# Written slots for the experts' steps of a fused graph-attention and expert layer, and an earlier read of the edge records

## The chip, the core and the metric

The kernel runs on one core of a Trainium2 chip. A core has five engines with an instruction queue each: TensorE (PE, matrix products; its weight loads are counted apart as PEld), VectorE (DVE), ScalarE (ACT), GpSimd (POOL) and SyncE (SP), which here issues most DMAs. Each engine works through its queue in order and waits on semaphores for the others. The metric is the time of one execution on the device, in microseconds; the median of three runs before the change is 6651.61 us (6647.99 to 6666.63).

## The reference

There are N = 30,000 nodes with 256 features and E = 510,000 edges, sorted by destination, each with a type out of 8. One layer is computed:

```
xn   = layernorm(x)
feat = einsum('ni,rhid->rnhd', xn, conv_weights)          # 8 types, 4 heads of 64
e    = leaky_relu(sum(feat[type, src] * attn_l[type]) + sum(feat[type, dst] * attn_r[type]))
h    = segment_softmax(e by dst)-weighted segment_sum of feat[type, src], + h_bias
x    = x + h
y    = layernorm(x)
x    = x + shared(y) + experts(y)
```

`shared` is a network of three layers (256, 128, 256 wide, relu between). `experts` are four networks of three layers (128, 64, 256 wide); a gate picks two of the four for each node by softmax, and their outputs are added with the softmax of the two gate values as weights.

## The kernel before

**The head.** It goes over the nodes in tiles of 128. For each tile VectorE and ScalarE normalise it, TensorE transposes it (`turn`, L292) and multiplies it by all 2048 columns of the weights, plus 64 columns for the attention terms, in pieces of 448 columns (`group`, L305). ScalarE and VectorE copy the pieces out of PSUM (L307), and SP stores a row of 32 x 65 values for each node in `feat` (L319). VectorE's copy of the transposed tile (L294) is what TensorE needs for the tile after the next few pieces.

Between two pieces, twice a tile, `aside()` runs one step of a list of generators: `edge_records` packs source, destination and type of all edges into `rec`; `places` reads these records back, in 21 batches of 12 blocks (`fetch`, L511), sorts out for each partition of a block a first edge, prepares flags and gather indices, and stores them; `expert_weights` loads the experts' weights. A generator gives its turn back at each `yield`. In `places` the first batch is fetched (L522), there is one `yield`, and then the loop fetches batch k + 1 and works on batch k, beginning with VectorE's `key` (L534). A fetch is, for each block, a load of its first edge's number into a register of SP and a DMA that uses it. From three quarters of the tiles on, `first_rows` gathers the first edge's row of each partition of all blocks ahead of time.

**The gather stage.** Edges are cut into 252 blocks of at most 2048 (16 for each of 128 partitions) and a last one of 18 x 128, each of which covers at most 128 destination nodes. For a block GpSimd gathers the edges' rows of `feat`, one indirect DMA for each of 15 places (18 in the last block) and all 128 partitions (L933), into a ring of four blocks in SBUF. There are 3798 such gathers. A gather into a place of the ring waits until TensorE's sums of the block that was there four blocks before are done.

The loop (L1124 to L1169) goes over steps t; a step is cut into NCH = 6 chunks c. In a step the work of several blocks is interleaved: `load` for block t + 2 and `gather` for t + 1 are issued at c = 0; `dest_expand` (TensorE, L987) and `dest_pick` (VectorE, L998 and L1000) bring the destinations' attention terms to block t + 1's edges; `scores` (c = 1), `turn_ends`, `across`, `turn_back` (c = 2, 3, 4), `softmax` and `exps` (c = 5) make block t's softmax; `weigh` (VectorE, L1079) multiplies block t - 1's rows by it, a chunk ahead of `sums` (TensorE, L1086), which adds up the rows by destination through one-hot matrices that ScalarE makes (`onehot`, L1010 and L1011); `finish` (L1104) waits for the sums of c = 5 in that same chunk; `residual_sum` of block t - 2 at c = 0 adds x.

**The experts.** Four blocks of results form a group (T = 4). When its fourth is there, the group's list of steps (`Experts.steps`, L713) is appended to the list `todo`, and each chunk of the loop takes one step from its front (L1157). The 22 steps of a full group, in order: `spread` (the root of the variance, ScalarE); two of `scale` (VectorE); two of `turn` (four transposes on TensorE each, L742, and a copy by ScalarE, L744); `shared1(0)`, `gates`, `shared1(1)`; four of `experts1`, of which the first begins with `choose`, some fifteen small VectorE operations that pick the two experts; `shared2`; two of `experts2`; two of `weigh` (transposes on TensorE, a product on VectorE); `turn_gates`; four of `last` (16 matrix products in all, a sum on VectorE and a store by SP for each). A layer is four instructions of 512 columns on TensorE (L798) and a relu on ScalarE (L799). A step may return a piece that is run at the start of the next chunk, through the list `late`. A group lasts 24 chunks, so before the change steps lie in chunks 0 to 21 of it, and 22 and 23 are free.

The order inside each engine's queue is the order in which this Python code calls the instructions (`manual_schedule`); no scheduler moves them.

Of the kernel before, what the change touches and what calls it, by code (L numbers as in the profile page):

```python
# [40 lines left out]
T = 4  # L41
# [12 lines left out]
def kernel(  # L54
# [121 lines left out]
    for i in range(NPEN + 1):  # L176
        f = wf.tile([P, H, U if i < NPEN else UL], F32, name=f"penf{i}")
# [44 lines left out]
    with ExitStack() as cx:  # L222
# [268 lines left out]
        def places(cl):  # L491
# [19 lines left out]
            def fetch(k):  # L511
                if k == len(batches):
                    return
                b0, n = batches[k]
                rc = rcs[k] = kp.tile([P, GB, UW, 4], I32, name="rcb")
                for b in range(n):
                    lo = nc.values_load(lo_sb[0:1, b0 + b:b0 + b + 1], engines={SP}, min_val=0, max_val=E)
                    r = rec[ds(lo, CAP), :].rearrange("(p u) f -> p (u f)", u=U)
                    nc.sync.dma_start(rc[:, b].rearrange("p u f -> p (u f)"),
                                      bass.AP(tensor=r.tensor, offset=r.offset, ap=[[4 * U, P], [1, 4 * UW]]))  # L520

            fetch(0)  # L522
            yield
            done = None
            for k, (b0, n) in enumerate(batches):
                fetch(k + 1)
# [99 lines left out]
        with tc.manual_schedule():  # L626
# [27 lines left out]
            while slot < 16:  # L654
                attention(slot, ab)
                slot += 1
            cl.close()
            side = [edge_records(cl), places(cl), expert_weights()]
            ahead = first_rows()

# [41 lines left out]
    class Experts:  # L702
# [8 lines left out]
        def steps(self):  # L711
            return ([self.spread] + [lambda j=j: self.scale(j) for j in (0, 2)]
                    + [lambda k=k: self.turn(k) for k in range(2)]  # L713
                    + [lambda: self.shared1(0), self.gates, lambda: self.shared1(1)]
                    + [lambda e=e: self.experts1(e) for e in range(NE)]
                    + [self.shared2] + [lambda i=i: self.experts2(i) for i in range(2)]
                    + [lambda i=i: self.weigh(i) for i in range(2)]
                    + [self.turn_gates] + [lambda t=t: self.last(t) for t in range(self.n)])

        def stats(self, t):  # L720
            st = self.pool.tile([P, 6], F32, name="c_st")
            nc.vector.bn_stats(st[:M], self.x1[:M, t, :])
            nc.vector.bn_aggr(self.mv[:M, t, :], st[:M])
# [138 lines left out]
    with ExitStack() as cx:  # L862
# [16 lines left out]
        NCH = 6  # L879
# [207 lines left out]
                                 s.ft[:, u].rearrange("p h d -> p (h d)"), start=u == 0, stop=u == s.u - 1)  # L1087

        groups = {}
        todo = []  # L1090
        late = []

        def put(t, rows_t):

            if t < NBLK:
                n0 = nc.values_load(n0_sb[0:1, t:t + 1], engines={SP}, min_val=0, max_val=N - P)
                nc.sync.dma_start(out[ds(n0, P), :], rows_t)
            else:
                nc.sync.dma_start(out[N - P:N, :], rows_t)
# [9 lines left out]
        def residual_sum(t):  # L1109
            s = blk.pop(t)  # L1110
            q, j = divmod(t, T)
            n = min(T, NBLK + 1 - q * T)
            if j == 0:
                x1 = x1p.tile([P, T, D], F32, name="x1")
                groups[q] = Experts(xc, ph_p, pc_p, x1, n, lambda i, r, q=q: put(q * T + i, r))
            x1 = groups[q].x1
            nc.vector.tensor_add(x1[:, j, :], s.ho.rearrange("p h d -> p (h d)"), s.xt)
            groups[q].stats(j)
            if j == n - 1:
                todo.extend(groups.pop(q).steps())  # L1120

        with tc.manual_schedule():  # L1124
            for t in range(-2, NBLK + 12):
                def at(f, b, *a):
                    if 0 <= b <= NBLK:
                        f(b, *a)
                for c in range(NCH):
                    while late:  # L1130
                        late.pop()()
                    if c == 0:
                        at(load, t + 2)
                        at(gather, t + 1)
                        at(flags, t + 1)
                    if c == 1:
                        at(flags_across, t + 1)
                    if c == 2:
                        at(turn_ends, t)
                    if c == 3:  # L1140
                        at(across, t)
                    if c == 4:
                        at(turn_back, t)
                    if c == 5:
                        at(softmax, t)
                        at(exps, t)
                    if c < NCH - 1:
                        at(weigh, t - 1, c + 1)
                    if c < 4:
                        at(dest_pick, t + 1, c)  # L1150
                    if c == 0:
                        at(residual_sum, t - 2)
                    if c == 1:
                        at(scores, t)
                    if c == 4:
                        at(dest_select, t + 2)
                    if todo:  # L1157
                        after = todo.pop(0)()
                        if after:
                            late.append(after)  # L1160
                    if c == 5:
                        at(weigh, t, 0)
                        at(dest_expand, t + 2, 0)
                    if c < 3:
                        at(dest_expand, t + 1, c + 1)
                    at(onehot, t, c)
                    at(sums, t - 1, c)
                    if c == 5:
                        at(finish, t - 1)  # L1169
            assert not todo and not groups and not late  # L1170


    again = nc.values_load(bad[0:1, 0:1], min_val=0, max_val=1)
# [187 lines left out]
    with ExitStack() as cx:  # L1361
# [3 lines left out]
        with tc.For_i(0, again * NQ) as q:  # L1365
# [7 lines left out]
            for step in g.steps():  # L1373
                after = step()
# [30 lines left out]
```

## Time and profile before

| | us |
|---|---|
| timed, median of 3 | 6651.61 |
| profiled execution | 8380.65 |
| its span | 8379.0 |
| last matrix product of the head ends | 1746 |
| first gather of the gather stage starts | 1750.45 |
| last gather starts | 8259.83 |

| engine | busy us in the span | share |
|---|---|---|
| TensorE | 6330.2 | 76% |
| VectorE | 5381.4 | 64% |
| GpSimd | 4073.5 | 49% |
| ScalarE | 3416.7 | 41% |

The profile is of one execution, and this one took 1729 us longer than the timed median. Its mean granted TensorE clock is 0.877. Busy time is the time in which an engine had an instruction running; the ends of matrix products are modelled. In lines of instructions in order of time the columns are start, duration (both us), engine, source line, operation, output and inputs, count, and in brackets the idle time before it with what ended it; "issue" stands for a wait that the profile doesn't explain, "remote" for one whose signal isn't matched to an instruction. In a row of a group, what stands behind the bar is busy time, mean ns of one instruction, idle time of the engine just before them, and what ended most of it. In the table of waits the columns are the total in us, how often, and the longest.

### The profile page before, as it was taken

What the parts mean: (1) busy time and instruction counts of PE and PEld (TensorE: products, weight loads), DVE (VectorE), ACT (ScalarE), POOL (GpSimd) and SP (SyncE); (2) the same over time, 40 slices, a digit from 0 to 9 for tenths busy, and PEclk for the clock granted to TensorE, in tenths of its full rate; (3) what the DMA queues carried; (4) which work ended last, traced back from release to release, by engine and by line L of the source; (5) the groups of instructions that cost most, each with busy time, mean ns of one, the idle gap of its engine ahead of it and who ended that gap; (6) DMA issues with size and microseconds to landing.
All of it is one profiled execution on the core that took longest, in us unless ns stands there. A gap on an engine that the chain in (4) does not pass through costs nothing. (4 is left out here: it accounts for less than half of the span.)

```text
span 8379.0 us, 96556 instructions
## 1 busy us (share of the span) xinstructions
PE 6330.2 (76%) x25254; PEld 3986.0 (48%) x25255; DVE 5381.4 (64%) x13882; ACT 3416.7 (41%) x9511; POOL 4073.5 (49%) x4327
## 2 busy tenths in 40 slices
PE   9999999956666767777666667777666777777667
PEld 5555555534444444444444444444444444444444
DVE  5557774447666666666666666666666666666665
ACT  2222222224444444444444444444444444444444
POOL 1101114665555555555555555555555555555552
PEclk9999999978888888888888888888888888888888
DMA  6657778964444444444444444444444444444441
GB/s 226 229 177 238 224 243 303 341 197 123 116 117 117 118 116 119 119 121 119 117 120 117 119 116 118 118 123 118 118 116 117 118 119 118 116 119 117 115 118 55
DMA packets 761457, 1209.52 MB, mean 144 GB/s; under 512 B 241638, under 2 KB 599789, under 8 KB 730685
## 3 DMA queue, kind: packets, MB, share of 16 engines
q1 hardware_dynamic: 565453, 663.56, 24.8%
q0 software_dynamic: 194400, 539.40, 23.3%
q8 instruction: 206, 3.38, 0.2%
q14 instruction: 358, 2.93, 0.1%
q10 hardware_dynamic: 1040, 0.26, 0.0%
HBM read 818.57 MB, written 384.23 MB: 144 GB/s over the span
## 5 line engine op out<-in xcount | busy, mean ns | idle before, releaser
L933 POOL DMA_INDIRECT ft<-feat,rk x3798 | 3608.6, 950 | 2919.9 <-PE po L1086 956.0
L1086 PE MATMUL po<-ft,oh 128*128 128x260 f32 x8100 | 2305.4, 421 | 286.3 <-DVE ho L1107 149.5
L1086 PEld LDWEIGHTS po<-ft,oh 128*128 128x128 f32 x8100 | 1565.4, 208 | 569.7 <-issue 292.4
L305 PE MATMUL ps<-w,xT 128*128 128x448 f32 (+1 forms) x4700 | 1712.6, 519 | 14.3 <-DVE xT L294 8.6
L1079 DVE TENSOR_TENSOR ft<-ft,p 128x768 f32<-128x768 f32 x1518 | 1289.9, 850 | 394.8 <-issue 184.1
L1010 ACT ACTIVATE oh<-icol,rk 128x128 f32<-128x128 f32 x4032 | 1329.1, 389 | 66.4 <-remote 45.5
L305 PEld LDWEIGHTS ps<-w,xT 128*128 128x128 f32 x4700 | 877.3, 191 | 704.9 <-issue 613.5
L798 PE MATMUL ph<-xT,w 128*128 128x512 f32 (+1 forms) x512 | 372.1, 859 | 961.8 <-issue 888.7
L307 ACT COPY fo<-ps 128x448 f32<-128x448 f32 (+1 forms) x711 | 377.3, 533 | 1087.4 <-PE ps L305 912.4
L998 DVE TENSOR_TENSOR ere<-pe,rk 128x384 f32<-128x384 f32 x1008 | 553.3, 549 | 373.4 <-remote 247.9
L1011 ACT ACTIVATE oh<-oh 128x384 f32<-128x384 f32 x1518 | 740.2, 488 | 49.4
L987 PEld LDWEIGHTS <-ohT 128*128 128x128 bf16 x4050 | 393.9, 158 | 548.8 <-issue 438.1
L798 PEld LDWEIGHTS ph<-xT,w 128*128 128x128 f32 x512 | 112.3, 260 | 1112.1 <-issue 952.5
L744 ACT COPY xT<-ph 128x512 f32<-128x512 f32 (+1 forms) x128 | 73.1, 572 | 1325.3 <-remote 1299.9
L1000 DVE TENSOR_REDUCE e<-ere 128x16 f32<-128x384 f32 (+1 forms) x1012 | 561.5, 555 | 34.8
L987 PE MATMUL pe<-erp,ohT 128*128 128x96 bf16 x4050 | 442.3, 236 | 113.3 <-DVE ohT L970 73.5
L798 PE MATMUL ph<-xT,v 128*128 128x512 f32 (+1 forms) x1024 | 500.2, 613 | 2.3 <-ACT h L799 1.5
L1062 DVE TENSOR_TENSOR c<-t,rk 128x128 f32<-128x128 f32 x252 | 71.8, 285 | 618.9 <-remote 582.0
L1071 ACT ACTIVATE p<-e 128x64 f32<-128x64 f32 (+1 forms) x253 | 70.4, 278 | 844.9 <-DVE e L1022 741.8
L307 DVE COPY fo<-ps 128x448 f32<-128x448 f32 (+1 forms) x464 | 242.3, 528 | 221.9 <-PE ps L305 194.2
L1040 PE MATMUL t<-ident,fb 128*4 128x128 f32 x253 | 70.8, 280 | 383.6 <-DVE fb L1033 196.7
L851 PE MATMUL pf<-w,h 128*128 128x256 f32 x506 | 203.2, 491 | 189.1 <-ACT wT L844 85.1
(206 smaller groups left out, 7422.2 us busy)
## 6 DMA issues: line engine op xcount, KB each, us to landing
feat<-fo SPq DMA_DIRECT2D x234, 1040.0 KB
dr<-dk_d SPq DMA_DIRECT2D x252, 516.0 KB
ft<-feat,rk POOLq DMA_INDIRECT x3798
stage<-fr SPq DMA_DIRECT2D x63, 520.0 KB
ft<-stage SPq DMA_DIRECT2D x252, 130.0 KB
xt<-xb_d SPq DMA_DIRECT2D x253, 128.0 KB
out_dram<-og SPq DMA_DIRECT2D x253, 128.0 KB
xb_d<-xb SPq DMA_DIRECT2D x58, 512.0 KB
```

The costliest lines, as they stand in the source:

```text
L305: nc.tensor.matmul(ps, t["xT"][:, k, :], w[:, k, c0:c1], start=k == 0, stop=k == 1)
L307: eng(t["fo"][:, h0:h1, :HD], ps[:, :n].rearrange("p (a d) -> p a d", d=HD))
L798: nc.tensor.matmul(ps[:, :self.w], lhs, rhs, start=i == 0, stop=i == len(pairs) - 1)
L851: nc.tensor.matmul(pf[:M], self.h2[:, tok], w3, start=True, stop=False)
L933: nc.gpsimd.indirect_dma_start(out=s.ft[:, u].rearrange("p h d -> p (h d)"), out_offset=None, in_=feat[:, :], in_offset=bass.IndirectOffse ...
L987: nc.tensor.matmul(pe[:, u - u0].rearrange("p f r -> p (f r)"), s.ov[:, u, :], s.erp.rearrange("n h k r -> n (h k r)"), start=True, stop=True)
L998: nc.vector.tensor_mul(ere, s.pe[:, :u1 - u0], s.th[:, u0:u1, None, :].to_broadcast([P, u1 - u0, H * 3, R]))
L1000: nc.vector.tensor_reduce(s.e[:, :, u0:u1].rearrange("p h u -> p u h"), ere.rearrange("p u (h k) r -> p u h (k r)", h=H), AX.X, ALU.add)
L1010: nc.scalar.activation(s.oh[:, u, :], icol, AF.Abs, bias=s.nd[:, u:u + 1])
L1011: nc.scalar.activation(s.oh[:, u0:u1], s.oh[:, u0:u1], AF.Relu, bias=1.0, scale=-1.0)
L1079: nc.vector.tensor_mul(fc, fc, pc[:, :, None].to_broadcast([P, (u1 - u0) * H, HD]))
L1086: nc.tensor.matmul(s.po.rearrange("n h d -> n (h d)"), s.oh[:, u, :], s.ft[:, u].rearrange("p h d -> p (h d)"), start=u == 0, stop=u == s. ...
```

## The change

Three edits:

- `places` gives its turn back six times instead of once between the fetch of the first batch and the first use of its records.
- A group's steps are no longer taken from a list one by one. `Experts.SLOTS` names a chunk for each of the 22 steps, counted from the chunk in which the group is complete. The chunks 3, 6, 17, 20, 22 and 23 have no step of this group. The four steps of the last layer are in chunks 24 to 27, which are chunks 0 to 3 of the next group: in 0, 1 and 2 they share the chunk with that group's `spread` and two `scale`, behind these. `plan` holds for each chunk of the loop the steps that are due; `free` keeps a later group (the last one, of a single block) from starting before 24 chunks have passed since the one before it.
- The pieces in `late` are run first in, first out instead of last in, first out.

```diff
@@ places
             fetch(0)
-            yield
+            for _ in range(6):
+                yield
             done = None
@@ class Experts
+        SLOTS = (0, 1, 2, 4, 5, 7, 8, 9, 10, 11, 12, 13, 14, 15, 16, 18, 19, 21, 24, 25, 26, 27)
+
@@
         groups = {}
-        todo = []
+        plan = {}
         late = []
+        free = [0]
@@ residual_sum
             if j == n - 1:
-                todo.extend(groups.pop(q).steps())
+                first = free[0] = max((t + 2) * NCH, free[0])
+                free[0] += T * NCH
+                for i, f in zip(Experts.SLOTS, groups.pop(q).steps()):
+                    plan.setdefault(first + i, []).insert(0, f)
@@ the loop
                     while late:
-                        late.pop()()
+                        late.pop(0)()
@@
-                    if todo:
-                        after = todo.pop(0)()
+                    for f in plan.pop(t * NCH + c, ()):
+                        after = f()
                         if after:
                             late.append(after)
@@
-            assert not todo and not groups and not late
+            assert not plan and not groups and not late
```

## The prediction

> **What bounds the kernel now.** I read the page first, then the stages, then GpSimd's instructions in order of time, then who waited for whom.
>
> The page: span, engines, and the costliest group.
>
> ```profile
> span 8379.0 us, 96556 instructions
> PE 6330.2 (76%) x25254; PEld 3986.0 (48%) x25255; DVE 5381.4 (64%) x13882; ACT 3416.7 (41%) x9511; POOL 4073.5 (49%) x4327
> L933 POOL DMA_INDIRECT ft<-feat,rk x3798 | 3608.6, 950 | 2919.9 <-PE po L1086 956.0
> ```
>
> No engine is full over the whole span, and the profiled execution (8380.65 us) is 1729 us longer than the timed median (6651.61). So before anything is costed, I must know where those 1729 us are. The row of L933 tells: 3798 gathers, each 0.95 us busy, and 2919.9 us of idle time in front of them. GpSimd's own instructions in order of time show how much of that idle time belongs to the gather itself:
>
> ```profile
> 1750.45 0.95 POOL L933 DMA_INDIRECT ft<-feat,rk  x1 [18.19 <-DMA stage<-fr]
> 1751.70 0.95 POOL L933 DMA_INDIRECT ft<-feat,rk  x1 [0.30 <-issue]
> 1752.96 0.95 POOL L933 DMA_INDIRECT ft<-feat,rk  x1 [0.30 <-issue]
> ...
> 8258.58 0.95 POOL L933 DMA_INDIRECT ft<-feat,rk  x1 [2.06 <-PE po L1086]
> 8259.83 0.94 POOL L933 DMA_INDIRECT ft<-feat,rk  x1 [0.30 <-issue]
> ```
>
> Nothing delays the second and third, and they start 1.25 us after the one before: 0.95 us and 0.30 us of issue. First to last gather is 8259.83 - 1750.45 = 6509 us; 3797 x 1.2525 = 4756 us of it is gathers without a wait, 1754 us is waiting. That is the missing 1729 us, within 25. So the timed execution has next to none of these waits: gather stage = 4756 us of GpSimd issue + about 25 us. With the head (1750 us) and the tail (8379 - 8260 = 119 us) as profiled, 1750 + 4756 + 119 + 2 around the span = 6627; the rest to 6651.6 is those 25 us. If the tail is shorter when timed (it holds some of the stalls below; 80 us would be my estimate), the waits left are up to 64 us.
>
> The waits that inflate the profile sit behind the experts' transposes. The table of waits:
>
> ```profile
> ACT xT L744 <- remote: 1299.9, 63, 22.3
> PE ph L798 <- issue: 889.1, 60, 16.7
> DVE c L1062 <- remote: 582.0, 61, 20.3
> ```
>
> 63 is the number of groups of four blocks: once a group ScalarE waits about 20 us for a transpose whose record ended long before. If that were in timed runs too, a group would take what it takes in the profile (6509 / 252 x 4 = 103.3 us); timed it is (6651.6 - 2 - 1750 - 119) / 252 x 4 = 75.9 us. VectorE alone is busy 4209.33 us of the 6300 between 1900 and 8200, or 69.0 us a group; with two waits of some 10 us in front of it (582 / 61, and those on PSUM at L998) it would be at 83. So these stalls belong to the profiled execution.
>
> The head is another regime. The busy time by stages (columns: stretch, its length, busy us and instructions of TensorE, its weight loads, VectorE, ScalarE, GpSimd; then granted clock, DMA share, GB/s):
>
> ```profile
> 570.00:580.00 10.00, 3.93 (x12) 1.90 (x10) 0.38 (x1) 0.19 (x1) 0.00 (x0) 0.94 0.17 31
> 580.00:590.00 10.00, 7.48 (x17) 3.77 (x18) 9.13 (x24) 1.94 (x5) 0.00 (x0) 0.72 0.16 30
> 590.00:600.00 10.00, 10.00 (x32) 5.58 (x31) 6.68 (x20) 2.44 (x6) 4.33 (x8) 1.00 0.82 313
> ```
>
> TensorE, then VectorE, in order of time at this gap:
>
> ```profile
> 569.68 4.25 PE L305 MATMUL ps<-w,xT 128*128 128x448 f32 x12
> 582.52 4.81 PE L305 MATMUL ps<-w,xT 128*128 128x448 f32 x8 [8.60 <-DVE xT L294]
> ...
> 579.62 0.50 DVE L534 SCALAR_TENSOR_TENSOR key<-rcb,iu 128x192 f32<-128x192 int32 x1 [12.35 <-DMA rcb<-rec]
> ```
>
> Else TensorE is busy 10.00 of 10 us at clock 1.00: it sets the head. Here VectorE stands 12.35 us at the first use of the records that `fetch(0)` reads, the copy of xT (L294) is queued behind, and TensorE runs dry for 8.60 us and comes back at a clock of 0.72.
>
> **What the Trainium skill says.** "DMA: Bandwidth & Descriptors", SWDGE vs HWDGE vs iDMA: descriptors of DMAs issued from GpSimd are computed by its own cores in software. The trace agrees: 0.95 us of GpSimd for each gather, whatever else runs. "Perfetto Trace Analysis", Tensor Engine Instruction: the end of a matmul's record is an estimate, not an observation; that fits ScalarE's wait of 20 us after a transpose that looks finished. "TensorE: Matmul & The Clock Gate", Part 1: TensorE's clock falls to half after an idle window of some 3.4 us; the stage above shows 0.72 after the gap of 8.60 us.
>
> **The change part by part.**
>
> Records six steps ahead. Nothing is added to any queue; the first batch's VectorE work comes five steps later than before, so the fetches of batch 1 on SP do too. Steps come twice a tile and a tile of the head takes 7.31 us (transposes at 547.53, 554.84, 562.15), so the first batch reaches VectorE 2.5 x 7.31 = 18 us later, from about 571 to 589. Its records are there at 579.6: cover of 9 us. Gain: 8.60 us of idle, and the slow restart (8 records in 4.81 us where 20 take 7.26, so 4.81 - 2.90 = 1.91). Together 10.5 us, and all of it reaches the end, since TensorE is full to its last matmul (1746) and the first gather starts at 1750.45, behind the last store. Bounds: 10.5 gained, or 0 if the wait only goes to another DMA. Everything after shifts by 18 us: the batches end near 1280 instead of 1262, the expert weights' loads near 1330, and TensorE is still busy with the head until 1746, so the cost is nothing; if that cover were gone it would be those 18 us.
>
> The experts' slots. 22 steps a group before and after, with the same instructions: spread, scales at slots 0, 1, 2 as before; the transposes go from 3, 4 to 4, 5; the first layer from 5 to 7; the last layer's four steps from 18 to 21 to 24 to 27, which are slots 0 to 3 of the next group. No gather moves, and nothing is put in GpSimd's queue. SP's stores of the output move with the last layer by six slots, so they stay at the same four places inside a step, behind the loads for the block two ahead that are issued at its start; a store that waits on VectorE there can hold up only the next step's loads, which have a whole step of 18.8 us in hand. So the path (60 gathers x 1.2525 = 75.2 us a group) loses and gains nothing directly. What it can lose is only waits: a gather waits until the sums of the block four before are done (ring of four blocks). Those are the 25 us (at most 64) of the timed run. What the slots do to the engines behind: the last layer (TensorE 1.7 us a step by its 8 records of some 0.22 us) now lies beside the scales (VectorE 0.41 x 4 = 1.65 us), slots heavy on one engine beside slots heavy on the other; and slot 5, where `finish` waits on VectorE for the sums of the same slot, has a transpose (0.44 us at that pace) in place of a 512 wide layer (1.9 us). I estimate 1 to 2 us a group less waiting on VectorE, in work that mostly follows GpSimd. I take 40% of the 25 us: 10 us gained. Bounds: 64 gained (every wait goes), and a loss as under the rivals.
>
> The order in which late pieces are run (first in, first out) changes nothing while one waits at a time, as here. The tail: the last groups run 36 steps after the blocks' work instead of 35, but four pairs of them overlap: 0, within 3 us.
>
> Sum: 6651.6 - 10.5 - 10 = 6631 us.
>
> **Rivals.**
>
> Compute and not GpSimd sets the timed pace. For it: VectorE's 69.0 us a group plus four waits for the exponentials (the timeline shows 1.7 us in front of the first weighting) come to 75.8, as near to the measured 75.9 as GpSimd's 75.2. Against it: the waits of the profile account for the whole difference only if they are nearly absent when timed. Then the slots' 1 to 2 us a group count up to GpSimd's limit, 0.7 us a group or 45 us, at most 64: 6651.6 - 10.5 - 45 = 6596.
>
> Slower: the doubled slots. In slot 1 VectorE now has the late sum of the last layer (0.42), weighting (0.68), pick (1.10), scores (1.75) and scale (0.83), and TensorE's next last layer waits for that late sum, since its PSUM tile has one buffer. If this delays transposes of scores, then `across`, softmax, the exponentials and the sums that free the ring, the group grows. GpSimd hides it until the group passes 75.2 us, from 72.6 (69.0 and 3.6 of small gaps, my estimate); beyond 2.6 us every us costs 63. At 3.4 us: +50, less 10.5: 6691.
>
> No difference: the wait on the first records turns into one on the next batch, and the ring hides the slots: 6651.
>
> **How the numbers follow.** GpSimd's pace with the head's gap gone: 0.45, 6615 to 6645 with 6631 in it. Compute's pace: 0.20, 6580 to 6615. Slower: 0.20, 6660 to 6710. No difference: 0.15, 6645 to 6658. About 0.3% (20 us) is what a measurement of this kernel can tell from no change; the three runs before lie within 18.7 us. Faster by more than that is below 6631.7: half of the first case and the second, 0.43. Slower is above 6671.6: most of the third, 0.18. Between: 0.39. The range of 8 in 10, 6590 to 6690, leaves out the ends of the second and third case.
>
> **What would show it.** In the profile after: TensorE has no gap between 560 and 600 us; the first gather starts near 1740; gathers without a wait still start 1.25 us apart; the time from the last gather to the end stays within 10 us of 119. The waits behind transposes can shrink or move by hundreds of us in the profiled execution; by my reading the timed median doesn't follow. If it follows, or falls under 6580, GpSimd is not what paces the timed run and the step on the 1729 us is wrong. If the median is over 6670, the doubled slots have passed the ring's cover.

## The result and the profile after

| | us |
|---|---|
| timed after, median of 4 (6773.13 to 6776.68) | 6774.7 |
| timed before, median of 4 (6647.99 to 6666.63) | 6652.67 |
| ratio | 1.018, interval 1.0162 to 1.0198 |
| profiled execution after | 6775.31 |
| its span | 6773.6 |

The change makes the kernel 1.8% slower; 6631 was predicted, with a range from 6590 to 6690. The profile of before that stands further up is of an execution that took 8380.65 us, so what is compared here is a second profile of the same kernel (the first experiment below), with a span of 6669.8 us, which is called undisturbed.

From the page of after: the span, the engines, and the costliest group (busy us and mean ns; then idle time in front of it).

```profile
span 6773.6 us, 96498 instructions
PE 5995.3 (89%) x25254; PEld 3855.3 (57%) x25255; DVE 5344.5 (79%) x13882; ACT 3435.3 (51%) x9511; POOL 4068.8 (60%) x4327
L938 POOL DMA_INDIRECT ft<-feat,rk x3798 | 3605.6, 949 | 1349.2 <-issue 448.8
```

The same three lines of the kernel before, undisturbed:

```profile
span 6669.8 us, 96556 instructions
PE 6002.1 (90%) x25254; PEld 3849.3 (58%) x25255; DVE 5352.6 (80%) x13882; ACT 3425.9 (51%) x9511; POOL 4069.6 (61%) x4327
L933 POOL DMA_INDIRECT ft<-feat,rk x3798 | 3606.7, 950 | 1236.2 <-issue 446.6
```

No engine's busy time differs by more than 10 us, and TensorE's mean granted clock is 0.963 in both. What has grown is the idle time in front of the gathers: 113 us more (1349.2 against 1236.2). The first gather starts 12 us earlier, and from the last gather to the end it takes 3 us longer, which makes the 104 us between the two spans. The gathers are where the loss shows; the runs below tell that it doesn't come from them. The table of waits (total us, times, longest us), first of after, then of the kernel before:

```profile
ACT xT L749 <- PE ph L747: 446.4, 65, 11.2
DVE ft L1084 <- ACT ft L1077: 370.7, 253, 2.2
POOL ft L938 <- PE po L1091: 320.0, 866, 4.1
```

```profile
POOL ft L933 <- PE po L1086: 305.6, 1003, 0.3
ACT xT L744 <- PE ph L742: 192.6, 65, 10.2
DVE ft L1079 <- ACT ft L1072: 181.3, 253, 1.0
```

VectorE waits for the exponentials once a block in both (253 blocks), but 370.7 us in all instead of 181.3. That is 189 us more, on the engine with the most work after TensorE. ScalarE also waits longer for the transposes (446.4 against 192.6), and one of these longer waits stands in front of an exponential, as the next lines show.

The gap of the head is gone. The busy time by stages (columns as in the prediction), after:

```profile
570.00:580.00 10.00, 10.00 (x31) 5.36 (x30) 5.36 (x17) 3.02 (x7) 0.47 (x1) 1.00 0.26 70
580.00:590.00 10.00, 10.00 (x31) 5.52 (x31) 5.39 (x17) 1.90 (x4) 0.00 (x0) 1.00 0.81 304
```

TensorE is busy 10.00 of 10 us at clock 1.00 where it had 4.57 and 6.80 us in the undisturbed kernel before. The first gather starts at 1733.3 us instead of 1745.4 ("near 1740" was reckoned from the 1750.45 of the first profile).

**Where VectorE's wait grows.** In every fourth block (the one whose chunk 4 is slot 4 of the group), instructions in order of time of after: TensorE, then VectorE, then ScalarE.

```profile
3422.54 0.69 PE L859 MATMUL pf<-b,wT 17*128 17x256 f32 x2
3424.68 0.22 PE L1060 MATMUL t<-ident,carf 4*128 4x4 f32 x1
3424.89 0.66 PE L747 MATMUL ph<-ident,c_xn 128*128 128x128 f32 x4
...
3420.88 0.38 DVE L1053 TENSOR_TENSOR_SCAN carb<-through,t 4x128 f32<-4x128 f32 x1
3424.20 1.28 DVE L975 TENSOR_SCALAR ohT<-dr,rowid 128x2064 bf16<-128x2064 int16 x1
3427.09 0.22 DVE L1027 TENSOR_REDUCE e<-m 128x4 f32<-128x64 f32 x1
3429.54 0.95 DVE L1084 TENSOR_TENSOR ft<-ft,p 128x768 f32<-128x768 f32 x1 [2.22 <-ACT ft L1077]
...
3425.58 0.59 ACT L749 COPY xT<-ph 128x512 f32<-128x512 f32 x1 [6.79 <-PE ph L747]
3426.07 0.98 ACT L1015 ACTIVATE oh<-icol,rk 128x128 f32<-128x128 f32 x3
3427.08 0.53 ACT L1016 ACTIVATE oh<-oh 128x384 f32<-128x384 f32 x1
3427.63 1.28 ACT L1076 ACT_TABLE_LOAD   x1
3428.92 0.28 ACT L1076 ACTIVATE p<-e 128x64 f32<-128x64 f32 x1
```

VectorE has the scores less their maximum (L1027) at 3427.31, the end of that line. ScalarE is not ready for them: it has waited 6.79 us for the transposes, then copies them, makes one-hot matrices and loads the table of the exponential, in the order of its queue, and starts the exponential at 3428.92. VectorE stands 2.22 us. The same place in the kernel before:

```profile
3403.73 0.22 PE L1055 MATMUL t<-ident,carf 4*128 4x4 f32 x1
3403.94 0.66 PE L742 MATMUL ph<-ident,c_xn 128*128 128x128 f32 x4
...
3402.34 0.38 DVE L1048 TENSOR_TENSOR_SCAN carb<-through,t 4x128 f32<-4x128 f32 x1
3405.13 1.28 DVE L970 TENSOR_SCALAR ohT<-dr,rowid 128x2064 bf16<-128x2064 int16 x1
3408.02 0.22 DVE L1022 TENSOR_REDUCE e<-m 128x4 f32<-128x64 f32 x1
3408.95 0.95 DVE L1079 TENSOR_TENSOR ft<-ft,p 128x768 f32<-128x768 f32 x1 [0.71 <-ACT ft L1072]
...
3404.63 0.58 ACT L744 COPY xT<-ph 128x512 f32<-128x512 f32 x1
3406.67 1.28 ACT L1071 ACT_TABLE_LOAD   x1
3408.27 0.28 ACT L1071 ACTIVATE p<-e 128x64 f32<-128x64 f32 x1 [0.32 <-DVE e L1022]
```

The same chain on ScalarE is there, and as long: from the transposes at 3403.94 to the exponential at 3408.27 it takes 4.3 us, against 4.0 after. But here VectorE comes to its part later still, and ScalarE waits for it (0.32). What has moved is TensorE: it begins `turn_back` (L1060) 3.4 us after VectorE finished `across` (L1053; median over the groups), where it was 1.0 us before, since the last layer (L859) of the previous group now lies in the chunks just ahead. In that time VectorE gets ahead: its `dest_select` (L975) begins 0.48 us before `turn_back`, where it began 1.40 us behind it before. So from the start of `turn_back` VectorE needs only 2.6 us to the end of L1027, while the chain on ScalarE, which stands behind the same late `turn_back`, needs 4.2 us to reach the exponential.

The second place is the block whose chunk 4 is slot 16, where the change puts the second `experts2` (before: slot 14). ScalarE, then VectorE, after:

```profile
3466.03 0.69 ACT L830 ACTIVATE a<-ph,c 128x512 f32<-128x512 f32 x1
3466.61 0.61 ACT L834 COPY wide<-wt 128x512 f32<-128x512 f32 x1
3467.12 0.99 ACT L1015 ACTIVATE oh<-icol,rk 128x128 f32<-128x128 f32 x3
3468.14 0.52 ACT L1016 ACTIVATE oh<-oh 128x384 f32<-128x384 f32 x1
3468.57 0.27 ACT L1076 ACTIVATE p<-e 128x64 f32<-128x64 f32 x1
...
3466.82 0.22 DVE L1027 TENSOR_REDUCE e<-m 128x4 f32<-128x64 f32 x1
3469.18 0.95 DVE L1084 TENSOR_TENSOR ft<-ft,p 128x768 f32<-128x768 f32 x1 [2.14 <-ACT ft L1077]
```

The scores are there at 3467.04 (the end of L1027); a relu and a copy of 512 columns (0.69 and 0.61 us) have come into the queue in front of the one-hots and the exponential, which starts 1.53 us late.

Over all groups VectorE's wait for the exponentials, by the block's number modulo 4, is 0.72, 0.72, 0.71, 0.72 us in the kernel before and 0.72, 2.22, 0.87, 2.13 after: 3.07 us more a group. VectorE's time of a group, put together from its instructions, gaps under 0.3 us, and waits:

| kernel | busy | small gaps | waits | group |
|---|---|---|---|---|
| before, undisturbed | 68.60 | 3.41 | 4.61 | 76.6 |
| six yields, old list | 68.52 | 3.41 | 4.32 | 76.3 |
| after | 68.44 | 3.36 | 6.69 | 78.5 |

78.5 - 76.3 = 2.2 us a group (3.07 for the exponentials and 0.5 for the gates' product more, 1.2 for the last layer less, and 0.1 less of busy time and gaps). 63 x 2.2 = 140 us; measured between those two spans: 6773.6 - 6636.6 = 137 (6636.6 is the span of the run with six yields, below).

TensorE is nearly as busy as VectorE in this stage: between 1900 and 6300 us of the undisturbed kernel before, 87.8% against 89.5%. But VectorE waits for TensorE's products only 1.7 us of the 76.6 of a group, while TensorE stands idle 7.4 us for VectorE and 1.9 for ScalarE. No run takes work from either of the two. That VectorE and not TensorE sets the pace rests on these waits, and on the last two runs, in which VectorE is held up or not while TensorE's work stays the same.

### The profile page after: what moved, and what is told of

Read it like the earlier page. It is cut to its first block, busy times and chain, and to the rows that moved or that the text cites. A ratio compares the mean times of both kernels' runs of the same rounds, so it can differ in the third digit from the quotient of the medians.

```text
span 6773.6 us, 96498 instructions
## 1 busy us (share of the span) xinstructions
PE 5995.3 (89%) x25254; PEld 3855.3 (57%) x25255; DVE 5344.5 (79%) x13882; ACT 3435.3 (51%) x9511; POOL 4068.8 (60%) x4327
## 5 line engine op out<-in xcount | busy, mean ns | idle before, releaser
L938 POOL DMA_INDIRECT ft<-feat,rk x3798 | 3605.6, 949 | 1349.2 <-issue 448.8
L1091 PE MATMUL po<-ft,oh 128*128 128x260 f32 x8100 | 2236.4, 411 | 343.0 <-ACT ends L960 169.6
L1091 PEld LDWEIGHTS po<-ft,oh 128*128 128x128 f32 x8100 | 1513.7, 201 | 728.8 <-ACT ends L960 351.9
L1084 DVE TENSOR_TENSOR ft<-ft,p 128x768 f32<-128x768 f32 x1518 | 1288.7, 849 | 370.7 <-ACT ft L1077 370.7
L1016 ACT ACTIVATE oh<-oh 128x384 f32<-128x384 f32 x1518 | 740.4, 488 | 48.1
L803 PE MATMUL ph<-xT,v 128*128 128x512 f32 (+1 forms) x1024 | 482.2, 594 | 1.9 <-ACT h L804 1.5
L992 PE MATMUL pe<-erp,ohT 128*128 128x96 bf16 x4050 | 426.2, 230 | 53.9 <-DVE ohT L975 48.1
L294 DVE COPY xT<-ptr 128x256 f32<-128x256 f32 x229 | 97.0, 424 | 370.6 <-PE ptr L292 368.7
L804 ACT ACTIVATE h<-ph,b 128x512 f32<-128x512 f32 x192 | 131.0, 682 | 433.2 <-PE ph L803 430.4
L616 POOL DMA_INDIRECT fr<-feat,lowc x252 | 239.2, 949 | 171.2 <-issue 68.9
L975 DVE TENSOR_SCALAR ohT<-dr,rowid 128x2064 bf16<-128x2064 int16 (+1 forms) x253 | 324.1, 1281 | 3.4 <-DMA feat<-fo 2.9
L803 PE MATMUL ph<-xT,w 128*128 128x512 f32 (+1 forms) x512 | 311.7, 743 | 0.2 <-ACT xT L749 0.2
L274 POOL TENSOR_TENSOR xb<-xg,hb 128x1024 f32<-128x1024 f32 (+1 forms) x59 | 141.8, 2403 | 276.6 <-DMA xg<-in_x_dram 162.0
L749 ACT COPY xT<-ph 128x512 f32<-128x512 f32 (+1 forms) x128 | 74.6, 584 | 446.4 <-PE ph L747 446.4
```

The costliest lines, as they stand in the source:

```text
L803: nc.tensor.matmul(ps[:, :self.w], lhs, rhs, start=i == 0, stop=i == len(pairs) - 1)
L938: nc.gpsimd.indirect_dma_start(out=s.ft[:, u].rearrange("p h d -> p (h d)"), out_offset=None, in_=feat[:, :], in_offset=bass.IndirectOffse ...
L975: nc.vector.tensor_scalar(ohT[:, :3 * s.dw].rearrange("n (i e) -> n i e", i=3), s.dr[:, :, :s.dw], rowid[:, t:t + 1], None, op0=ALU.is_equal)
L992: nc.tensor.matmul(pe[:, u - u0].rearrange("p f r -> p (f r)"), s.ov[:, u, :], s.erp.rearrange("n h k r -> n (h k r)"), start=True, stop=True)
L1016: nc.scalar.activation(s.oh[:, u0:u1], s.oh[:, u0:u1], AF.Relu, bias=1.0, scale=-1.0)
L1084: nc.vector.tensor_mul(fc, fc, pc[:, :, None].to_broadcast([P, (u1 - u0) * H, HD]))
```

## The experiments

Theory A, formed on these traces: VectorE's queue paces the gather stage, and GpSimd's 75.2 us a group lie just below it. What ScalarE or TensorE have in chunk 4 ahead of the exponentials lengthens it. Theory B is that of the prediction: GpSimd paces, with room for VectorE, or (its slower rival) the doubled slots, those with steps of two groups, cost as such.

### The kernel before, and the head alone

First, before without any edit. 

> The kernel before, unchanged, for a second profiled execution. Theory A (the 20 us behind the transposes belonged to that one execution, and in the timed runs VectorE and GpSimd are close to each other): the span falls to about 6650 us, once a group no wait of 20 us is left, and VectorE is busy or in front of the weighting of the exponentials nearly all the time, in 75.6 us a group. Rival B (the long waits belong to the kernel under the profiler): the span is again near 8380 us.

Measured 6671.49 us, with the profile shown above. Its gathers take 4823.3 us from the first to the last, 67.6 more than 3797 x 1.2525. The 1754 us of waits that the prediction read from its profile are not in an undisturbed execution.

```diff
@@ before, places
-            yield
+            for _ in range(6):
+                yield
```

> The kernel before with the records read six steps ahead alone. The first gather of the changed kernel starts at 1733 us and not 1750, so if the head is independent of the experts' slots: 6653 - 17 = 6636 us. If the head's gap was part of the disturbed execution only: 6653 us.

Measured 6649.68 against 6660.79, ratio 0.9985 (0.9979 to 0.9992): 11 us gained. The head's part of the prediction (10.5) holds; the 17 us of the expectation were reckoned from the first gather of the first profile.

```diff
@@ after, places
-            for _ in range(6):
-                yield
+            yield
```

> The changed kernel with a single step between the first fetch and its use, so the slots alone. If the two parts add up, and the slots cost all of the loss: 6775 + 10 to 17 = 6785 to 6792 us. If the earlier read costs something in the gather stage, less than 6775 us.

Measured 6785.25, ratio 1.0187 (1.017 to 1.0204). The slots alone cost 124 us; less the 11 us of the head that is 113, and the change, against the same 6660.79, costs 114. The two parts add up.

### Which slots

```diff
@@ after
-        SLOTS = (0, 1, 2, 4, 5, 7, 8, 9, 10, 11, 12, 13, 14, 15, 16, 18, 19, 21, 24, 25, 26, 27)
+        SLOTS = (0, 1, 2, 4, 5, 7, 8, 9, 10, 11, 12, 13, 14, 15, 16, 17, 18, 19, 20, 21, 22, 23)
```

> The changed kernel with slots 0, 1, 2, 4, 5 and then 7 to 23 without a hole: free slots behind the scales and the transposes, the last layer in 20 to 23, nothing beside the next group's first steps. Theory A (ScalarE late for the exponentials: the second experts2 stands at chunk 4, with a relu and a copy in front of the exponentials, and VectorE waits there 2.13 us where 0.72 is the least, in one block of four, some 90 us in all): slow as the changed kernel, 6720 to 6775 us. Theory B (the doubled slots 0 to 3 cost): fast, 6630 to 6660 us.

Measured 7119.71, ratio 1.0687 (1.0669 to 1.0705), which neither theory had expected. The table of waits of this kernel names a new one, VectorE's sum waiting for the last layer's product:

```profile
DVE og L862 <- PE pf L859: 362.6, 191, 9.2
DVE ft L1084 <- ACT ft L1077: 269.2, 253, 2.2
```

The wait for the exponentials at slot 4 is down to 0.72 us although the transposes are in slots 4 and 5 as in the change; only the one at slot 16 stays (2.12). TensorE begins `turn_back` there 0.4 us after `across`. So the wait at slot 4 needs both, transposes there and the last layer ahead of them. But the last layer in chunks 2 to 5 of the fourth block costs much more (a group of 84.1 us, 5.5 of it in the wait of the first line). Why TensorE is so late with it was not tried further and stays open.

```diff
@@ after: the second experts2 out of chunk 4
-        SLOTS = (0, 1, 2, 4, 5, 7, 8, 9, 10, 11, 12, 13, 14, 15, 16, 18, 19, 21, 24, 25, 26, 27)
+        SLOTS = (0, 1, 2, 4, 5, 7, 8, 9, 10, 11, 12, 13, 14, 15, 17, 18, 19, 21, 24, 25, 26, 27)
```

> The changed kernel with its second experts2 in slot 17 in place of 16, so behind the exponentials of chunk 5 on ScalarE and not before them. Theory A (ScalarE is late for the exponentials in two of four blocks, and VectorE, which has no slack, pays): the wait in front of the first weighting of that block falls from 2.13 to 0.72 us, 1.41 us x 63 groups = 89 us: 6775 - 89 = 6686 us, the other late block stays at 2.22. Rival (the doubled slots set the loss, or GpSimd does): 6755 to 6795 us.

Measured 6723.73, ratio 1.0095 (1.0076 to 1.0114), 51 us less than after where A had 89. The wait at slot 16 fell from 2.13 to 0.83, nearly as expected, but `gates` waits for its product 0.6 us a group longer (1.10 against 0.53), and the group is 77.6 us; 0.6 x 63 = 38 us is what is missing from the 89. Why that wait grew is not shown.

```diff
@@ after: the transposes back to 3 and 4
-        SLOTS = (0, 1, 2, 4, 5, 7, 8, 9, 10, 11, 12, 13, 14, 15, 16, 18, 19, 21, 24, 25, 26, 27)
+        SLOTS = (0, 1, 2, 3, 4, 7, 8, 9, 10, 11, 12, 13, 14, 15, 16, 18, 19, 21, 24, 25, 26, 27)
```

> The changed kernel with the two transposes in slots 3 and 4 as in the kernel before. Theory A1 (the slot number of the transposes makes ScalarE late): the wait of 2.22 us falls to 0.72, 1.5 x 63 = 95 us: 6680 us. Theory A2 (TensorE is late in slot 4 because the last layer now stands in slots 0 to 3, so the second transposes' copy still stands late in front of the exponentials): the wait stays near 2.2 us, and the time at 6760 to 6790 us.

Measured 6785.47, ratio 1.019 (1.0171 to 1.0209), 11 us more than the change. One of the two transposes is still in chunk 4, and the waits are 2.22 and 2.12 as in the change.

```diff
@@ after: transposes at 3 and 5, the second experts2 at 17
-        SLOTS = (0, 1, 2, 4, 5, 7, 8, 9, 10, 11, 12, 13, 14, 15, 16, 18, 19, 21, 24, 25, 26, 27)
+        SLOTS = (0, 1, 2, 3, 5, 7, 8, 9, 10, 11, 12, 13, 14, 15, 17, 18, 19, 21, 24, 25, 26, 27)
```

> The changed kernel with the transposes in slots 3 and 5 and the second experts2 in 17, so that no step of slots 4 and 16 has work on ScalarE in front of the exponentials; the last layer stays beside the next group's first steps. Theory A: both waits fall to 0.72 us, 2.9 us a group: 78.5 - 2.9 = 75.6 us a group, 6775 - 183 = 6592 us, under the kernel with six yields alone (6650). If the doubled slots cost by themselves: 6650 to 6700 us.

Measured 6621.34, ratio 0.9938 (0.9919 to 0.9958). With chunk 4 clear in both blocks the waits are 0.72, 0.73, 0.90 and 0.83 us and the loss becomes a gain, though 29 us short of what was expected: a group takes 76.1 us and not 75.6, and 0.55 us of it is VectorE waiting for the last layer's product, which the change didn't have.

```diff
@@ after: the old list of steps, only the last layer moved
-        SLOTS = (0, 1, 2, 4, 5, 7, 8, 9, 10, 11, 12, 13, 14, 15, 16, 18, 19, 21, 24, 25, 26, 27)
+        SLOTS = (0, 1, 2, 3, 4, 5, 6, 7, 8, 9, 10, 11, 12, 13, 14, 15, 16, 17, 24, 25, 26, 27)
```

> The changed kernel with slots 0 to 17 without holes, as before the change, and only the last layer moved to 24 to 27. Theory A2: the second transposes in slot 4 come late behind the last layer of slots 0 to 3, VectorE waits some 1.5 us longer for the exponentials there, and saves the 1.2 us a group that it waits for the last layer before: +0.3 us a group, 6650 + 20 = 6670 us. If moving the last layer is free of cost: 6650 - 77 = 6573 to 6595 us. If the doubled slots cost all of the loss: 6775 us.

Measured 6669.65, ratio 1.0019 (1.0012 to 1.0025). Against the six yields alone, the overlap with a transpose left in slot 4 costs 20 us: the wait there is 2.22 again, the others 0.72. TensorE begins `turn_back` 3.85 us after `across`, with nothing but the last layer moved.

### Is it GpSimd, and is it the place in ScalarE's queue?

```diff
@@ six yields, old list: one gather a block left out, from the fifth block on
-            for u in range(1 if s.own else 0, s.u):
+            for u in range(1 if s.own else 0, s.u - (s.own and t >= RING)):
```

> The kernel with six yields (old list of steps), in which each block from the fifth on leaves out the gather of its last place; that place keeps what an earlier block left in the ring, so the sums are those of wrong rows, while every other instruction stays. 248 gathers less, 248 x 1.2525 = 311 us of GpSimd's issue, and 3.75 us less in front of each block. If GpSimd's gathers pace the timed stage (the prediction's step on the 1729 us): 6650 - 311, about 6340 us, or down to where VectorE's 68.5 + 3.4 us a group come next. If VectorE's queue with its waits for the exponentials paces it (theory A): the time stays, 6635 to 6655 us, with GpSimd idle near 26 us a group in place of 21.

```diff
@@ the last layer over (as above): the second transposes and all between one chunk later
-        SLOTS = (0, 1, 2, 3, 4, 5, 6, 7, 8, 9, 10, 11, 12, 13, 14, 15, 16, 17, 24, 25, 26, 27)
+        SLOTS = (0, 1, 2, 3, 5, 6, 7, 8, 9, 10, 11, 12, 13, 14, 15, 16, 17, 18, 24, 25, 26, 27)
```

> The changed kernel with the slots 0, 1, 2, 3, 5, 6 ... 18, 24, 25, 26, 27: the last layer overlaps as in the change, the second transposes leave slot 4 (free), the second experts2 is at 15, not in the fifth chunk of a block. Theory A (VectorE's queue, lengthened when ScalarE's or TensorE's work of chunk 4 stands in front of the exponentials): all four waits for the exponentials fall to 0.72 us, the late sums of the last layer wait less, a group takes 75.3 to 76.0 us against 76.6 of before, so 6585 to 6625 us. Doubled slots as such are the cost (the prediction's rival): no better than the change, 6740 us or more. If GpSimd's 75.2 us a group is the floor it can't go under 6585 us.

Beside these two the kernel before took 8441.34 us in seven timed runs (8428.21 to 8442.98), about as long as the execution that the prediction read; the two kernels took 8339.04 (0.9858, 0.9817 to 0.99) and 8340.2 (0.9878, 0.9859 to 0.9898). The expectations were for 6660 us of before, so neither can be judged by these times. Both kernels were run again, on another chip.

> The same kernel as in the run on which the kernel before took 8441 us: six yields, old list of steps, the gather of the last place left out from the fifth block on (the sums there are those of wrong rows). Where the kernel before takes some 6660 us: if GpSimd's gathers pace the stage, 6650 - 311 = 6340 us or down to VectorE's need; if VectorE's queue with its waits for the exponentials paces it, the time stays at 6635 to 6655 us.

Measured 6654.21 against 6660.88, ratio 0.999 (0.9981 to 1.0); with six yields and all gathers it is 6649.68. 311 us of GpSimd's work are gone and the time stays. The page's row of the gathers, and their wait in the table of waits:

```profile
L934 POOL DMA_INDIRECT ft<-feat,rk x3550 | 3371.9, 950 | 1457.8 <-issue 407.6
```

```profile
POOL ft L934 <- PE po L1087: 397.0, 912, 8.3
```

From the first gather to the last it takes 4809.7 us, with all gathers 4804.0. In excess of 1.2525 us a gather that is 364.6 us instead of 48.3: GpSimd now waits for about as long as it no longer works, up to 8.3 us at a time in the line shown. GpSimd doesn't pace this stage.

> The slots 0, 1, 2, 3, 5, 6 ... 18, 24 to 27 once more. Theory A (VectorE's queue; ScalarE's or TensorE's work of chunk 4 ahead of the exponentials lengthens it): all four waits at 0.72 us, a group of 75.3 to 76.0 us, 6585 to 6625 us. Doubled slots as such are the cost: 6740 us or more. A floor by GpSimd is at 6585 us.

Measured 6581.16, ratio 0.9882 (0.9865 to 0.9898): 80 us under the kernel before and 193 under the change, with the change's three doubled slots (0, 1 and 2) and a fourth, slot 3, beside them. All four waits for the exponentials are 0.72 to 0.75 us. ScalarE where the chain was late, and VectorE's line in the table of waits:

```profile
3440.91 1.28 ACT L1076 ACT_TABLE_LOAD   x1
3443.43 0.28 ACT L1076 ACTIVATE p<-e 128x64 f32<-128x64 f32 x1 [1.24 <-DVE e L1027]
```

```profile
DVE ft L1084 <- ACT ft L1077: 183.8, 253, 1.6
```

ScalarE has the table loaded 1.24 us before VectorE is there, although TensorE begins `turn_back` as late as in the run with only the last layer moved (3.85 us after `across`): what is gone is the transposes and their copy behind it. Against the run with the last layer over and a transpose in slot 4 it is 88 us faster; the wait of 2.22 that became 0.73 is 1.5 x 63 = 94. And the gathers hardly wait any more: from the first to the last it takes 4760.7 us, 4.9 in excess of 1.2525 a gather. Here, and in no other of these runs, GpSimd is the bound. The time lies 4 us under the expected range and its floor: from the last gather to the end it takes 84.7 us, where the others take 99 to 108.

```diff
@@ six yields, old list: exps (junk is a tile in SBUF that nothing reads)
+            if t % 4 == 1:
+                for _ in range(3):
+                    nc.scalar.copy(junk.rearrange("p (i w) -> p i w", i=4), ident[:, None, :].to_broadcast([P, 4, P]))
             nc.scalar.activation(s.p, s.e.rearrange("p h u -> p u h"), AF.Exp)
             nc.scalar.copy(s.ft[:, :, :, HD], s.p)
```

> Six yields, old list of steps, and in one block of four three idle copies of 128x512 on ScalarE (0.48 us apart, 1.45 us) just ahead of the exponentials. No slot is touched. Theory A: ScalarE had 0.33 us to spare there, so VectorE's wait for the exponentials grows from 0.72 to about 1.85 us, the group by 1.1 us, the kernel by 63 x 1.1 = 70 us, to about 6720 us. If GpSimd paces with the 2.6 us of cover that the prediction gave: no change, 6650 us.

Measured 6769.96, ratio 1.017 (1.0153 to 1.0187). ScalarE there, in order of time:

```profile
3415.74 1.90 ACT L1075 COPY junk<-ident 128x512 f32<-128x512 f32 x3
3417.66 1.28 ACT L1076 ACT_TABLE_LOAD   x1
3418.96 0.28 ACT L1076 ACTIVATE p<-e 128x64 f32<-128x64 f32 x1
```

The copies took 1.90 us, not 1.45, so the wait of that block is 2.13 us instead of 0.72. That of the next block is 1.48, which was not expected: there a relu of the experts and one-hots stand just ahead of the exponential, and why they come late now is not shown. Together 2.17 us a group, 63 x 2.17 = 137 us; measured 120 over the six yields.

```diff
@@ six yields, old list: exps
             nc.scalar.activation(s.p, s.e.rearrange("p h u -> p u h"), AF.Exp)
             nc.scalar.copy(s.ft[:, :, :, HD], s.p)
+            if t % 4 == 1:
+                for _ in range(3):
+                    nc.scalar.copy(junk.rearrange("p (i w) -> p i w", i=4), ident[:, None, :].to_broadcast([P, 4, P]))
```

> The same three copies just behind the exponentials and the copy of them in ScalarE's queue. ScalarE's work is that of the run with the copies ahead. Theory A: the exponentials come as early as before, so 6640 to 6665 us. If ScalarE's amount of work counted and not its place: as slow as with the copies ahead.

Measured 6651.94, ratio 0.9993 (0.9984 to 1.0001), all waits for the exponentials at 0.71 to 0.73 us. VectorE's wait for the exponentials with the copies ahead, then with the copies behind:

```profile
DVE ft L1084 <- ACT ft L1077: 315.9, 253, 3.3
DVE ft L1084 <- ACT ft L1074: 182.0, 253, 1.0
```

The same work on ScalarE costs 120 us ahead of the exponentials and 2 us behind them, with no slot touched: it is the place in the queue.

## Why the prediction was wrong

**What bounds the kernel: the step that failed.** "So the timed execution has next to none of these waits: gather stage = 4756 us of GpSimd issue + about 25 us." As a sum it was near: 67.6 us of waits in the undisturbed execution, where it took 25 and allowed 64. As a statement of what paces the stage it was wrong. That GpSimd waits little says only that whatever it waits for is little slower than itself. VectorE needs 76.6 us a group with the waits in its own queue, GpSimd 75.2, and leaving 311 us out of GpSimd's work changed nothing. The prediction had both numbers (75.2, and 75.8 under its rival, in which compute sets the pace), and let an equality within 25 us decide between two that lie 0.6 us a group, or 38 us, apart. That the rival's 75.8 comes so near to the 76.6 is luck: it took 1.7 us for each of the four waits for the exponentials, which take 0.72, and left out 3.4 us of small gaps and 1.7 of other waits.

**The cover of 2.6 us a group** follows from that step and wasn't there. 72.6 was VectorE's busy time and gaps, 72.0 as measured; but VectorE's waits, 4.6 us a group in the kernel before, were put down as following GpSimd. Those for the exponentials do not: 2.9 of the 4.6 us are four times the 0.72 us from VectorE's last operation through the exponential (0.28) and its copy (0.27) back to VectorE, whose next instruction in its queue needs them. There was no cover, so what the slots added to VectorE's group came to the end: 137 us of span for 2.2 us, or 62 for each, near the 63 that the prediction itself gives for what lies beyond the cover.

**Slots, nothing directly on the path; 1 to 2 us a group less waiting.** The less was there: the wait for the last layer's product, 1.2 us a group with six yields, is gone after. Missing was ScalarE. The part on the slots speaks of TensorE, VectorE, SP and GpSimd, and names nothing that is queued on ScalarE behind the moved copies and relus. There stands the exponential, for which VectorE waits: at slots 4 and 16 VectorE's wait grew by 1.50 and 1.41 us, and by 3.07 us a group over all four blocks.

**The slower rival** had the right sign, the right price (63) and the wrong place: slot 1, and the doubling as such. The run with four doubled slots at 6581 us shows that the doubling isn't what costs: it reaches GpSimd's bound, so what is left of such a cost would be hidden there. Slots 4 and 16 cost. Its forecast of 6691, and the sign "if the median is over 6670, the doubled slots have passed the ring's cover", fall with that. The rival in which compute sets the pace named the bound; its 6596 took only a gain from the slots, where the change brought a loss. Its number is near what the slots reach once the exponentials are left alone (6581).

**Records six steps ahead.** Right: 10.5 predicted, 11 measured, no gap between 560 and 600, the first gather 12 us earlier. Wait and gap were the same in the first profile (12.35 and 8.60 us) as in the undisturbed one (12.40 and 8.63).

**The 20 us behind the transposes.** That the timed 6651 us don't have them is right (10.2 us is the longest of 65 such waits in the undisturbed kernel before). But they are not the profiler's: beside two of the runs above, all timed runs of the kernel before took 8428 us or more. What sets them off is not shown, nor that the estimated ends of the matrix products' records have to do with them.

**The tail.** Within 10 us of 119 was expected; it is 104.2, and 101.1 in the undisturbed kernel before. So the change did little to it, and the 119 belonged to the execution of 8380.65 us.

The Trainium skill, "Perfetto Trace Analysis", Identifying the Most-Contended Engine, judges VectorE, ScalarE and GpSimd by the share of time in which they are busy. In the undisturbed kernel before that puts VectorE (80%) ahead of GpSimd (61%), and the run with a gather less agrees. In the run of 6581 us it fails: GpSimd paces with 62% against VectorE's 81%, because of 1.2525 us from one gather to the next only 0.95 are recorded as busy. "ScalarE: Activation LUTs", What ACT_TABLE_LOAD costs, has 1283 ns for the load of a table, and some 1380 ns more for a drain; the trace agrees on the load with 1.28 us, and shows nothing of the drain, since the load starts 0.02 us after the one-hots end and the exponential 0.01 us after the load ends (L1016 and L1076 above, in the profile of after). The load lies in ScalarE's queue ahead of the exponential, so it lengthened the chain after the late transposes, here as before.

## What to carry to other kernels

Before a step is moved, list for every engine, the idle one too, what will stand behind it in that engine's queue and who waits for that; ScalarE is busy half the time here, and 1.90 us of copies ahead of one exponential a group cost 120 us in 63 groups, or 1.9 us each, though none of VectorE's own work was touched. Two engines whose times for a period differ by one or two per cent can't be told apart by which one waits little: take work away from one of them and see whether the time follows. And where a profile's execution is longer than the timed ones, take another one before anything is read from its waits.

## What was not expected of the hardware

Where the long stalls stand depends on the kernel: behind the experts' transposes in the kernel before (63 waits, 22.3 us at the longest, in the execution of 8380.65 us), and behind the gates' product in the kernel with the fewest moves when it took 8340.2 us, where VectorE's wait at `gates` came to 671.3 us in 44 times. Their cause was not found. Three copies of 128x512 from SBUF on ScalarE took 1.90 us from the first to the last, where the prices read from copies out of PSUM (0.48 us apart) gave 1.45.
